# The end of a long convolution: statistics, sums and roundings moved between three engines

## The chip, the cores and the metric

The kernel runs on one core of a Trainium2 chip. A core has a matrix engine (TensorE, PE in the profile; PEld is its loading of weights), a vector engine (VectorE, DVE), a scalar engine (ScalarE, ACT), a general engine (GpSimd, POOL) and a sync engine (SyncE, SP) that issues most transfers. Each engine works through its own instructions in order and waits for others by semaphores. The metric is the device time of one execution in microseconds; less is better.

## The reference, cut to what matters

The model has two layers, each of a cross part and an FFN. The first cross part is a causal convolution over all pairs of features in a head, with `fft_size` twice the length; the change lies at its end and in the first tiles of the FFN after it.

```python
# k = v = ctx, q = layernorm(x); (8, 256, 512) each; 32 heads of 8 rows, length 512
kv  = einsum('bhil,bhjl->bijhl', k_, v_)
y   = irfft(rfft(kv, n=1024) * rfft(ssm_kernel, n=1024))[..., :512]
out = einsum('bijhl,bhil->bjhl', y + kv * D, q_)
x   = x + tanh(g_xattn[0]) * out
# FFN 0: weights rounded to -1, 0, 1 by their mean; activations to 8 bits by row maximum
h   = silu(bitlinear(layernorm(x), w1)) * bitlinear(layernorm(x), w2)
x   = x + tanh(g_ffn[0]) * bitlinear(h, w3)
# then attention over ctx under a mask, and FFN 1 (1-bit weights, activations in groups of 64)
```

`_weight_quant` is `clip(round(w / mean|w|), -1, 1)`; after the rounding the clip of an integer to [-1, 1] equals its sign.

## The kernel before

**The convolution** is done head by head, as a product with a Toeplitz matrix built by the transfers of `load_toep`. Loop variable `h` (lines 716 to 748) runs over the 32 heads; I call one turn a step. For each head the symmetric products of features (36 of 64 pairs) are made on GpSimd (`pair_products`, from the doubled copy that `ctx_twice` makes on ScalarE). TensorE then makes `y` in two halves of PSUM: (h,0) takes 6 matmuls in the trace and (h,1) takes 14. The halves go through a ring of three PSUM tiles (`ps_y`). `half_wrap` on ScalarE copies a few columns of `y` so that a row can be read cyclically; `half_products` on VectorE multiplies by `q` (three instructions, lines 348, 354, 361) into `prod`; `add_halves` on GpSimd adds the two planes of `prod` (line 371); `reduce_terms` on VectorE sums four terms (line 376) into `qT`, one step later. In four heads, `alone = {12, 14, 19, 21}`, GpSimd's adding is left out and VectorE sums all eight terms itself (line 378), in the head's own step.

In step h the order on VectorE is: products (h,1), sum of head h−1, sum of head h if it is lone, products (h+1,0), then the jobs of this step. TensorE makes (h+1,1), then (h+2,0), each into the PSUM tile that the products (h,0) and (h,1) set free.

**Jobs.** Other work is woven into the steps by `job(h, slot, ...)` and run by `run(h, slot)`; slots stand at fixed places of a step ("act", "dve", "pe", "act2", "pool", "late"). The scheduling is manual: program order is each engine's order. Of the jobs, these matter here:
- The rows of `x` are 16 tiles of 128. `ln_moments_of` takes mean and variance of a tile for the normalising of FFN 0, with two instructions on VectorE (lines 116, 117). Tiles are numbered by `order0`; numbers 4 to 7 have their statistics in steps 28 to 31, in slot "dve".
- For the first two tiles `front_norm`, `front_max`, `front_int` and `front_turn` prepare the FFN's input in steps 25 to 29: normalise (ScalarE, line 179), row maximum (VectorE, line 483), round to int8 (ScalarE, line 502), clip and cast (GpSimd, line 506) and a transposing transfer from SP's queue (line 508). The integers lie in one buffer, `i8x` in pool `front1`. In the FFN the same four are run two tiles ahead.
- The weights of FFN 0 are rounded in two passes. `round_w0` (ScalarE, line 447) makes int8 in a ring of three buffers (`pr`), and `clip_w0` (GpSimd, line 454) clips them to bf16. The last matrix has four pieces; they are rounded in steps 27 to 30 and clipped in steps 29, 30, 31, 31.

After step 31 ScalarE loads the table of Silu (line 189), and **FFN 0** (lines 920 to 1005) runs over the tiles t. `up_block` makes two products of 512, 512 and 384 columns in a ring of four PSUM tiles: `pa` is read by silu on ScalarE (line 800), `pb` by the gating on VectorE (line 801). One tile later the hidden row gets its row maximum (line 483), its integers (ScalarE, line 935), a cast on GpSimd (line 951) and a transposing transfer (line 953); two tiles later `down0` multiplies it by the third matrix (line 809). In tile 0, `ln_finish` (three small instructions on VectorE, fourteen on GpSimd) makes the inverse deviations for numbers 4 to 7, and the last head's sum is done at the tile's end (line 984). Its result is read by the transposes of `odd_back` from t = 1 on. Attention and FFN 1 follow and are not touched.

Of the kernel before, what the change touches and what calls it, by code (L numbers as in the profile page):

```python
# [9 lines left out]
F32 = mybir.dt.float32  # L10
BF16 = mybir.dt.bfloat16
F32R = mybir.dt.float32r
I8 = mybir.dt.int8
# [3 lines left out]
AF = mybir.ActivationFunctionType  # L17
ALU = mybir.AluOpType
# [3 lines left out]
P = 128  # L22
B, S, L = 8, 256, 512
NT = B * S // P
NL = L // P
H, HD = 32, 8
# [12 lines left out]
GRP = 4  # L39
# [3 lines left out]
def flamingo_gated_kernel(  # L43
# [15 lines left out]
    nc = tc.nc  # L59

    def pool(stack, name, bufs, **kw):
# [3 lines left out]
    small = pool(ctx, "small", 3)  # L65
# [10 lines left out]
    w0q = [  # L76
        wp_ab.tile([P, NL, FF0], BF16, name="w0_1"),
        wp_ab.tile([P, NL, FF0], BF16, name="w0_2"),
        wp_c.tile([P, NF0, L], BF16, name="w0_3"),
    ]  # L80
    pf = pool(s_front, "front", 2, side="right")
    pf1 = pool(s_front, "front1", 1, side="right")
# [14 lines left out]
    xs = const.tile([P, NT, L], F32, name="xs")  # L97
# [3 lines left out]
    order0 = evens + odds  # L101
# [11 lines left out]
    def ln_moments(mv, j, t):  # L113

        st = small.tile([P, nc.vector.BN_STATS_DIM], F32, tag="st", name="st")
        nc.vector.bn_stats(st, xs[:, t, :])
        nc.vector.bn_aggr(mv[:, j, :], st)
# [19 lines left out]
    def ln_moments_of(got, order, k, tag):  # L137

        g, j = k // GRP, k % GRP
        if g not in got:  # L140
            got[g] = small.tile([P, GRP, 2], F32, tag="mv" + tag, name="mv")
        ln_moments(got[g], j, order[k])

    def ln_finish(got, g, tag):

# [82 lines left out]
    big = pool(s_conv, "p1big", 1)  # L228
    p2 = pool(s_conv, "p1", 2)
# [24 lines left out]
    qT = big.tile([P, NL * B, S], F32, name="qT")  # L254
# [7 lines left out]
    toeps, chs, cxs, kvs, qxs, prods, ys = {}, {}, {}, {}, {}, {}, {}  # L262
# [71 lines left out]
    def half_wrap(h, half):  # L334
        y = ys[h, half]
        nc.scalar.copy(y[:, :, :, 0:W0], y[:, :, :, HD * ND : HD * ND + W0])  # L336
# [36 lines left out]
    def reduce_terms(h, added):  # L373
        prod, o = prods.pop(h), qT[:, :, h * HD : (h + 1) * HD]
        if added:
            nc.vector.tensor_reduce(o, prod[:, 0], AX.X, ALU.add)  # L376
        else:
            nc.vector.tensor_reduce(
                o, prod.rearrange("p k a j d -> p (a j) k d"), AX.XY, ALU.add
            )  # L380

    trs = {}

    def transpose_x(t, xn):
# [18 lines left out]
    FW = [[FF0] * NL, [FF0] * NL, [3 * L, 3 * L, 3 * L, 2 * L]]  # L403
# [37 lines left out]
    w0r = {}  # L441
# [9 lines left out]
    def clip_w0(i, k):  # L451
# [3 lines left out]
            q[:, a : a + n], w0r.pop((i, k))[:, :n], 1.0, -1.0, ALU.min, ALU.max  # L455
        )


    w1a = {}
    N1 = FF1 * L // P // 1024  # L460
# [17 lines left out]
    st0, xn0, i80, am0, x0 = {}, {}, {}, {}, {}  # L478
# [19 lines left out]
        am0[k] = row_max(xn0[k], "x")  # L498

    def front_int(k):  # L500
        i80[k] = pf1.tile([P, L], I8, tag="i8x", name="i8x")
        nc.scalar.activation(i80[k], xn0.pop(k), AF.Copy, scale=am0[k][1])

    def front_turn(k):
# [11 lines left out]
    def job(h, slot, f, *a):  # L516
        jobs.setdefault((h, slot), []).append((f, a))

    def run(h, slot):
        for f, a in jobs.pop((h, slot), []):  # L520
            f(*a)
# [49 lines left out]
    for i, (a, b, c) in enumerate(STEPS0):  # L571
        for k in range(NL):
            job(a + k, "load", load_w0, i, k)
            job(b + k, "act", abs_w0, i, k)
            job(c[k], "act", round_w0, i, k)
            job(c[k] if i < 2 else (29, 30, 31, 31)[k], "pool", clip_w0, i, k)
        job(b + NL - 1, "dve", total_w0, i)
        job(b + NL, "act", spread, i)
        job(b + NL, "dve", mean_w0, i)
    steps1 = [2, 7, 8, 9, 10, 12, 13, *range(15, 19), 18, 19, 20, 21, 23]  # L580
    for k, h in enumerate(steps1):
        job(max(h - 2, steps1[k - 2] if k > 1 else 0), "late", load_w1a, k)
        job(h, "act2", abs_w1, k)
        if k % N1 == N1 - 1:
            i = k // N1
# [8 lines left out]
    for k in range(2):  # L594
# [1 line left out]
        job(26 + k, "dve", front_max, k)  # L596
        job(27 + k, "act", front_int, k)
        job(28 + k, "pool", front_turn, k)
    for k in range(GRP, 2 * GRP):
        job(24 + k, "dve", ln_moments_of, st0, order0, k, "0")  # L600

# [111 lines left out]
    alone = {12, 14, 19, 21}  # L715
    for h in range(H):
        if h + 3 < H:
            load_toep(h + 3)
        if h + 4 < H:
            load_ch(h + 4)  # L720
        run(h, "load")
        if h + 1 < H:
            q_twice(h + 1)
        if h + 3 < H:
            ctx_twice(h + 3)
            pair_products(h + 3)
        half_products(h, 1)
        if h > 0 and h - 1 not in alone:
            reduce_terms(h - 1, True)
        if h in alone:  # L730
            reduce_terms(h, False)
        else:
            add_halves(h)
        if h + 1 < H:
            half_matmuls(h + 1, 1)
        run(h, "act")
        if h + 1 < H:
            half_wrap(h + 1, 1)
            half_products(h + 1, 0)
        run(h, "dve")  # L740
        if h + 2 < H:
            half_matmuls(h + 2, 0)
        run(h, "pe")
        run(h, "act2")
        if h + 2 < H:
            half_wrap(h + 2, 0)
        run(h, "pool")
        run(h, "late")
    assert not jobs
# [17 lines left out]
    p2 = pool(s_mid, "p2", 2, side="right", reuse_waits="tile")  # L767
# [48 lines left out]
    scale = 1.0 / math.sqrt(L)  # L816
# [103 lines left out]
    for t in range(NT + 1):  # L920
        new = t + 2 < NT
        if t < NT:
            hh = p2.tile([P, FF0], F32, tag="hh", name="hh")
        if new:
            front_norm(t + 2)
        if 1 <= t:
            inv, sc = row_max(h_[t - 1], "h")
        if t == NT:
            xT_ = {k: x_transposed(xn_.pop(k)) for k in range(2)}
            xn_[2] = normalised3(2)  # L930
        if t < NT:
            up_block(*x0[t], hh, 0)
        if 1 <= t:
            q = p1.tile([P, FF0], I8, tag="i8h", name="i8h")
            nc.scalar.activation(q, h_.pop(t - 1), AF.Copy, scale=sc)
        if t == NT - 1:
            xn_ = {k: normalised3(k) for k in range(2)}
        if t >= 3:
            residual(order0[t - 3], *d_.pop(t - 3))
        back = BACK.get(t, [])  # L940
        if len(back) == 3:
            sums.append(odd_back(odds[back[0]]))
        if new:
            front_max(t + 2)
        if t < NT:
            up_block(*x0[t], hh, 512)
        if new:
            front_int(t + 2)
        if 1 <= t:
            b = p2.tile([P, FF0], BF16, tag="qh", name="qh0")  # L950
            nc.gpsimd.tensor_scalar(b, q, 127.0, -128.0, ALU.min, ALU.max)
            bT = p_hq.tile([P, NF0, P], BF16, tag="hqT", name="hqT")
            nc.sync.dma_start_transpose(out=bT, in_=b)
            f3 = small.tile([P, 1], F32, tag="f3", name="f3")
            nc.gpsimd.tensor_scalar(f3, inv, gw0, None, ALU.mult)
            hq_[t - 1] = (bT, f3)
        if new:
            front_turn(t + 2)
        for add in sums:
            add()  # L960
        sums = []
        if back:
            sums.append(odd_back(odds[back[-2]]))
        if t >= 2:
            hqT, f3 = hq_.pop(t - 2)
            d_[t - 2] = (down0(hqT), f3)
        if t in FINISH:
            ln_finish(*FINISH[t])

        for k in STATS3.get(t, ()):  # L970
            ln_moments_of(st3, natural, k, "3")
        if t > 0:
            for k in STATS0.get(t, ()):
                ln_moments_of(st0, order0, k, "0")
        if t < NT:
            up_block(*x0.pop(t), hh, 1024)
            h_[t] = hh
        if back:
            sums.append(odd_back(odds[back[-1]]))
        for add in sums:  # L980
            add()
        sums = []
        if t == 0:
            reduce_terms(H - 1, True)
        if t == 3:
            s_conv.close()
            wp1 = pool(ctx, "w1", 1, reuse_waits="tile")
            w1q = [wp1.tile([P, NL, FF1], F32R, name=f"w1_{i + 1}") for i in range(2)]
            p_st = pool(s_att, "w1st", 3, reuse_waits="tile")
        if t == NT - 3:  # L990
            p3 = pool(s_att, "p3", 2, reuse_waits="tile")
            keys, values = {0: load_keys(0)}, {0: load_values(0)}
        for make in signs:
            make()
        signs = []
        if 3 <= t < NT:
            signs = [w1_signs(made + k) for k in range(2)]
            made += 2
        if t == NT - 2:
            bytes_ = {b: load_mask(b) for b in range(2)}  # L1000
        if t == NT - 1:
            negs = {0: key_mask(bytes_.pop(0))}
            gates3 = {0: batch_gate(negs[0])}
        if t == NT:
            negs[1] = key_mask(bytes_.pop(1))
# [90 lines left out]
    for t in range(NT + 2):  # L1096
# [11 lines left out]
        if t == NT:  # L1108
            xn4, q, back = front(1)
# [53 lines left out]
        if t == NT - 4:  # L1163
            ln_some(st4, natural, GRP, "4")
            xn4, q, back = front(0)
# [14 lines left out]
    with ExitStack() as ph:  # L1180
        p2 = pool(ph, "p4", 2, reuse_waits="tile")
# [92 lines left out]
        for t in range(NT):  # L1274
# [6 lines left out]
            if t > 0:  # L1281
                hh = px.tile([P, HW], F32, tag="hh", name="hh4")
                g = up_products(xT, 0)
# [4 lines left out]
                g = up_products(xT, 1)  # L1288
# [7 lines left out]
            g = up_products(xT, 2)  # L1296
# [5 lines left out]
            g = up_products(xT, 3)  # L1302
# [76 lines left out]
```

## Time and profile before

| | us |
|---|---|
| three runs | 744.36, 744.26, 742.74 |
| their median | 744.26 |
| the profiled execution | 743.63 |
| its span | 741.8 |
| mean granted clock of TensorE | 0.998 of full |

The span is what the profiler saw from the first to the last instruction; the execution's own time holds 1.83 us more around it. The convolution ends near 188 us, FFN 0 near 312, attention near 400, and FFN 1 takes the rest. The profile page's first part, busy time with its share of the span and the number of instructions:

```profile
PE 712.2 (96%) x3172; PEld 527.8 (71%) x3172; DVE 606.8 (82%) x1234; ACT 362.3 (49%) x638; POOL 255.9 (34%) x360
```

Of its second part, the row of GpSimd: 40 slices of the span, in tenths of a slice.

```profile
POOL 2888988988875435443200010000200002000000
```

GpSimd's work lies almost wholly in the first half, and in the convolution's slices it is nearly full. The page's average over the whole span hides this, as it hides any stage: the change touches only some steps between 80 and 206 us, and these have to be looked at by themselves.

### The profile page before, as it was taken

The numbers are of one execution on the slowest core, as the hardware profiler recorded it, in microseconds if no ns is written. First come the engines' busy times: TensorE is split into PE (matmuls) and PEld (weight loads), VectorE is DVE, ScalarE is ACT, GpSimd is POOL, SyncE is SP. The second block draws the span as 40 slices with busy tenths as digits, with TensorE's granted clock in tenths as the row PEclk, the third lists the DMA queues.
The fourth block names the chain that finished last, engine by engine and source line by source line (L and its number), as shares of the span: only waits on it lengthen the run. The fifth ranks groups of instructions, "written<-read, shape, count | busy, mean of one in ns | idle before, by whom it ended". The sixth has DMA issues, their size and how long they took to land.

```text
span 741.8 us, 10045 instructions
## 1 busy us (share of the span) xinstructions
PE 712.2 (96%) x3172; PEld 527.8 (71%) x3172; DVE 606.8 (82%) x1234; ACT 362.3 (49%) x638; POOL 255.9 (34%) x360
## 2 busy tenths in 40 slices
PE   4999999999899999899989999999999999999997
PEld 3777777776454444556657888888888888888885
DVE  5799878998888888877767999888889888778965
ACT  5477877756677886767742233222223322222322
POOL 2888988988875435443200010000200002000000
PEclk9999999999999999999999999999999999999999
DMA  5675775921145667686602555455534545553443
GB/s 193 224 230 169 183 263 190 287 79 31 22 89 135 151 139 173 152 278 192 206 35 46 109 123 124 90 114 110 115 85 105 113 92 123 109 111 85 109 88 85
DMA packets 150444, 99.36 MB, mean 134 GB/s; under 512 B 84280, under 2 KB 128312, under 8 KB 150392
## 3 DMA queue, kind: packets, MB, share of 16 engines
q1 hardware_dynamic: 149608, 98.38, 51.7%
q0 software_dynamic: 256, 0.26, 0.5%
q8 instruction: 25, 0.41, 0.2%
q14 instruction: 27, 0.22, 0.1%
q10 hardware_dynamic: 528, 0.08, 0.1%
HBM read 75.58 MB, written 5.03 MB: 109 GB/s over the span
## 4 chain that ended last, share of the span: by engine, by line
PE 64%; DVE 5%; DMA 2%; POOL 2%; issue 1%; ACT 1%; SPq 0%; DVEq 0%; POOLq 0%
PE po L1254 16%; PE pb L1076 15%; PE pa L1076 15%; PE po L809 5%; PE pb L792 4%; PE pa L792 4%; PE po L904 3%; PE ps L875 2%; DMA w1st<-in_L_w3t 1%; DMA sT<-d 1%; DMA hqT<-qh 1%; PE tr L867 1%; DVE qT L376 0%; DVE prod L348 0%; DMA w1st<-in_L_w2t 0%
## 5 line engine op out<-in xcount | busy, mean ns | idle before, releaser
L326 PE MATMUL y<-kv,toep 128*128 128x288 f32 x640 | 162.4, 410 | 4.0 <-DVE prod L361 2.7
L326 PEld LDWEIGHTS y<-kv,toep 128*128 128x128 f32 x640 | 120.2, 192 | 37.6 <-ACT qx L290 3.0
L1084 ACT ACTIVATE sl<-pa,wmean 128x512 f32<-128x512 f32 x64 | 44.0, 689 | 187.6 <-PE pa L1076 187.6
L1076 PE MATMUL pa<-w,hi 128*128 128x512 f32 x256 | 100.7, 393 | 0.0
L1254 PE MATMUL po<-w,lo 128*128 128x512 f32 x256 | 100.0, 391 | 0.0
L1076 PE MATMUL pb<-w,hi 128*128 128x512 f32 x256 | 99.8, 390 | 0.1
L1254 PE MATMUL po<-w,hi 128*128 128x512 f32 x256 | 99.7, 390 | 0.0
L1076 PE MATMUL pa<-w,lo 128*128 128x512 f32 x256 | 99.7, 389 | 0.0
L1076 PE MATMUL pb<-w,lo 128*128 128x512 f32 x256 | 99.7, 389 | 0.0
L159 POOL TENSOR_TENSOR nwt<-rstd 128x4 f32<-128x4 f32 x33 | 6.5, 198 | 247.2 <-DVE rstd L154 245.3
L303 POOL TENSOR_TENSOR kv<-cx 128x1024 f32<-128x1024 f32 x32 | 60.6, 1893 | 32.9 <-ACT cx L290 30.4
L371 POOL TENSOR_TENSOR prod<-prod 128x1024 f32<-128x1024 f32 x28 | 66.2, 2366 | 2.7 <-DVE prod L361 2.7
L792 PEld LDWEIGHTS <-xqT 128*128 128x128 bf16 x384 | 37.4, 97 | 41.5 <-issue 4.5
L1051 ACT CAST hi<-v 128x512 fp32r<-128x512 f32 x64 | 39.1, 622 | 48.0 <-DVE v L1244 48.0
L1088 DVE SCALAR_TENSOR_TENSOR hh<-pb,wmean,sl 128x512 f32<-128x512 f32 x64 | 47.7, 745 | 15.4 <-PE pb L1076 15.4
L1254 PEld LDWEIGHTS po<-w,lo 128*128 128x128 f32 x256 | 48.1, 188 | 10.8 <-DVE lo L1056 1.0
L1076 PEld LDWEIGHTS pb<-w,hi 128*128 128x128 f32 x256 | 48.0, 188 | 10.6 <-DVE hh L1088 0.5
L1076 PEld LDWEIGHTS pa<-w,hi 128*128 128x128 f32 x256 | 48.1, 188 | 10.4 <-issue 0.5
L1076 PEld LDWEIGHTS pa<-w,lo 128*128 128x128 f32 x256 | 48.1, 188 | 10.3 <-issue 0.5
L1076 PEld LDWEIGHTS pb<-w,lo 128*128 128x128 f32 x256 | 48.1, 188 | 10.0
L1254 PEld LDWEIGHTS po<-w,hi 128*128 128x128 f32 x256 | 48.0, 188 | 9.9
L348 DVE TENSOR_TENSOR prod<-y,qx 128x512 f32<-128x512 f32 x64 | 43.6, 681 | 10.7 <-ACT y L336 6.8
(141 smaller groups left out, 1327.3 us busy)
## 6 DMA issues: line engine op xcount, KB each, us to landing
sT<-d SPq DMA_DIRECT2D x64, 256.0 KB
toep<-ssm_skip SPq DMA_DIRECT2D x31, 256.0 KB
ch<-in_ctx_heads SPq DMA_DIRECT2D x32, 128.0 KB
w1a<-in_L_w1t SPq DMA_DIRECT2D x8, 512.0 KB
w1a<-in_L_w2t SPq DMA_DIRECT2D x8, 512.0 KB
w1st<-in_L_w1t SPq DMA_DIRECT2D x16, 256.0 KB
w1st<-in_L_w2t SPq DMA_DIRECT2D x16, 256.0 KB
cT<-in_ctx_t SPq DMA_DIRECT2D x8, 512.0 KB
```

The costliest lines, as they stand in the source:

```text
L303: nc.gpsimd.tensor_tensor(kv[:, :, 0 : ND * HD].rearrange("p a (i d) -> p a i d", d=ND), cx[:, :, 0:HD].unsqueeze(3).to_broadcast([P, NL * ...
L326: nc.tensor.matmul(y[:, k, :, W0 : W0 + NPAIR], toeps[h][:, d * P : (d + 1) * P], kvs[h][:, mi * B : (mi + 1) * B, :].rearrange("p b n -> ...
L348: nc.vector.tensor_tensor(prod[:, 0, r, :, :], yv[:, :, W0 : W0 + ND * HD].rearrange("p a (i d) -> p a i d", d=ND), view(q, [HX, n], [1, H ...
L371: nc.gpsimd.tensor_tensor(flat[0], flat[0], flat[1], ALU.add)
L792: nc.tensor.matmul(pp[:, :fw], xqT[:, c, :], w0q[i][:, c, f0 : f0 + fw], start=(c == 0), stop=(c == NL - 1),)
L809: nc.tensor.matmul(po, hqT[:, c, :], w0q[2][:, c, :], start=(c == 0), stop=(c == NF0 - 1))
L904: nc.tensor.matmul(po, eT[:, c, :], cN[:, c, :], start=(c == 0), stop=(c == S // P - 1))
L1051: nc.scalar.copy(hi, v)
L1076: nc.tensor.matmul(pp, xT[k][:, c, :], w1q[i][:, c, f0 : f0 + 512], start=(c == 0 and k == 0), stop=(c == NL - 1 and k == 1),)
L1084: nc.scalar.activation(sl, pa, AF.Silu, scale=wmean1[:, 0:1])
L1088: nc.vector.scalar_tensor_tensor(hh, pb, wmean1[:, 1:2], sl, op0=ALU.mult, op1=ALU.mult)
L1254: nc.tensor.matmul(po, hT[b][k][:, c, :], w1q[2][:, b * NL + c, :], start=(b == 0 and c == 0 and k == 0), stop=(b == NB - 1 and c == NL - ...
```

## The change

Five things are done.
1. The sum of a lone head moves one step later, to the place where other heads have theirs.
2. The integers of tile number 1 get a buffer of their own, in pool `p1big`.
3. The statistics of numbers 5, 6 and 7 are taken on ScalarE, in slot "late" of steps 29, 30 and 31: a pass that sums the row, a one-column scaling, a pass that sums squares of the deviations, two more one-column scalings. Number 4 stays on VectorE.
4. The last head's sum is done on GpSimd, in two additions, in step 31 after the adding of its halves and ahead of the step's clip; `prod`'s second plane holds the half sums.
5. The last piece of the last weight matrix is clipped on ScalarE as a sign, at the end of tile 0, in place of GpSimd in step 31.

```diff
+    def moments_by_act(got, order, k, tag, junk):
+        g, j = k // GRP, k % GRP
+        mean, var = got[g][:, j, 0:1], got[g][:, j, 1:2]
+        v = xs[:, order[k], :]
+        st = small.tile([P, nc.vector.BN_STATS_DIM], F32, tag="st", name="st")
+        nc.scalar.activation(junk, v, AF.Identity, accum_out=st[:, 0:1])
+        nc.scalar.activation(st[:, 1:2], st[:, 0:1], AF.Copy, scale=-1.0 / L)
+        nc.scalar.activation(junk, v, AF.Square, bias=st[:, 1:2], accum_out=st[:, 2:3])
+        nc.scalar.activation(mean, st[:, 0:1], AF.Copy, scale=1.0 / L)
+        nc.scalar.activation(var, st[:, 2:3], AF.Copy, scale=1.0 / L)
...
+    def reduce_last(h):
+        prod, o = prods.pop(h), qT[:, :, h * HD : (h + 1) * HD]
+        half = prod[:, 1, :, :, 0:2]
+        nc.gpsimd.tensor_tensor(half, prod[:, 0, :, :, 0:2], prod[:, 0, :, :, 2:4], ALU.add)
+        nc.gpsimd.tensor_tensor(o, half[..., 0], half[..., 1], ALU.add)
...
+    def clip_by_act(i, k):
+        n, a = FW[i][k], sum(FW[i][:k])
+        q = w0q[i].rearrange("p c f -> p (c f)")
+        nc.scalar.activation(q[:, a : a + n], w0r.pop((i, k))[:, :n], AF.Sign)
...
     def front_int(k):
-        i80[k] = pf1.tile([P, L], I8, tag="i8x", name="i8x")
+        i80[k] = (big if k == 1 else pf1).tile([P, L], I8, tag="i8x", name="i8x")
...
-            job(c[k] if i < 2 else (29, 30, 31, 31)[k], "pool", clip_w0, i, k)
+            if (i, k) != (2, 3):
+                job(c[k] if i < 2 else (29, 30, 31)[k], "pool", clip_w0, i, k)
...
-    for k in range(GRP, 2 * GRP):
-        job(24 + k, "dve", ln_moments_of, st0, order0, k, "0")
+    def first_by_act(k):
+        junk = p2.tile([P, L], F32, tag="xn", name="junk")
+        moments_by_act(st0, order0, k, "0", junk)
+
+    job(28, "dve", ln_moments_of, st0, order0, GRP, "0")
+    for k in range(GRP + 1, 2 * GRP):
+        job(24 + k, "late", first_by_act, k)
...
-        if h > 0 and h - 1 not in alone:
-            reduce_terms(h - 1, True)
-        if h in alone:
-            reduce_terms(h, False)
-        else:
+        if h > 0:
+            reduce_terms(h - 1, h - 1 not in alone)
+        if h not in alone:
             add_halves(h)
...
+        if h == H - 1:
+            reduce_last(h)
         run(h, "pool")
...
         if t == 0:
-            reduce_terms(H - 1, True)
+            clip_by_act(2, 3)
```

## The prediction

> **What bounds the kernel now.** I read the busy time by stage first, then the chain that ended last, then the timeline of the two stretches that the change touches. The rows by stage (window in us, its length, then busy us and count of PE, weight loads, DVE, ACT and POOL, granted clock, DMA share, GB/s):
>
> ```profile
> 82.00:128.00 46.00, 44.64 (x194) 34.71 (x193) 38.04 (x67) 35.69 (x66) 40.97 (x29) 1.00 0.69 217
> 128.00:171.00 43.00, 41.96 (x187) 32.83 (x185) 40.23 (x85) 29.80 (x55) 37.30 (x27) 1.00 0.56 171
> 171.00:188.00 17.00, 14.37 (x56) 10.06 (x56) 14.83 (x33) 9.26 (x15) 14.32 (x12) 1.00 0.15 31
> 188.00:206.00 18.00, 15.73 (x80) 7.86 (x79) 16.18 (x31) 11.11 (x18) 14.97 (x26) 1.00 0.23 36
> 206.00:312.00 106.00, 103.91 (x523) 52.24 (x524) 91.42 (x183) 81.91 (x115) 53.92 (x106) 1.00 0.61 138
> ```
>
> TensorE is full nearly everywhere; only 171 to 206, the convolution's end and the first tiles of the FFN, leaves it 4.9 us idle (17.00 − 14.37 plus 18.00 − 15.73). After 206 it has 2% of slack, so time won or lost before 206 goes through to the end. The chain of waits agrees: from 179 to 195 it is almost all DVE, from 206 all PE, and between them runs GpSimd, then the transpose of the first hidden tile (start, length, what):
>
> ```profile
> 199.51 0.23 POOL nmr L165
> 199.74 0.89 issue
> ...
> 200.68 1.36 POOL qh L951
> ...
> 202.06 4.05 DMA hqT<-qh
> ...
> 206.16 2.55 PE po L809 x11
> ```
>
> So 206.16 is the gauge: what moves it moves the end.
>
> **Part 1, lone sums in the next step.** A lone step now does two sums on DVE before it may do the products that free TensorE's next PSUM tile. The timeline (start, length, engine, line, in brackets the idle time before it):
>
> ```profile
> 87.02 1.22 DVE L376 TENSOR_REDUCE qT<-prod 128x256 f32<-128x1024 f32 x1 [1.06 <-POOL prod L371]
> 88.16 2.27 DVE L378 TENSOR_REDUCE qT<-prod 128x256 f32<-128x2048 f32 x1
> ...
> 91.86 9.94 PE L326 MATMUL y<-kv,toep 128*128 128x288 f32 x40 [1.13 <-DVE prod L361]
> 102.03 13.33 PE L326 MATMUL y<-kv,toep 128*128 128x288 f32 x54 [0.23 <-DVE prod L361]
> ```
>
> Step 12: with the 2.27 sum gone, products (13,0) start at 88.16 and end at 89.5; TensorE had been done at 85.72 + 5.02 = 90.74 and goes straight on: **1.13 won**. The sum lies in step 13 between products (13,1), 89.7 to 91.0, and (14,0), which then end at 94.5; TensorE wants them after 20 matmuls of 0.2485 from 90.74, at 95.71: no new stall. Step 14, alike: **0.23 won**; sum 14 in step 15 makes (16,0) end at 105.0, wanted at 105.65. Steps 19 and 21 hide stalls too (0.48 and 0.56 of PE idle at 128.76 and 140.14). But there DVE, 40.23 of 43.00 busy, has as much work as before and only one listed wait after 137 (0.28): I count nothing, and keep 0 to 1.0 for the range. No DMA moves by itself; the loads of a step follow its buffers. Part 1: −1.36, at worst −0.3 if a load of the context heads becomes late (cx waited 1.21 for one at 129.93).
>
> **Part 2, the tail**, in the old clock, part 1 taken off at the end. The rows that carry it:
>
> ```profile
> 178.10 0.72 ACT L502 ACTIVATE i8x<-xn,sc 128x512 int8<-128x512 f32 x1 [3.95 <-POOL qx L506]
> 179.07 0.69 DVE L348 TENSOR_TENSOR prod<-y,qx 128x512 f32<-128x512 f32 x1 [1.60 <-ACT y L336]
> 187.25 1.28 ACT L189 ACT_TABLE_LOAD   x1
> 189.36 0.67 ACT L800 ACTIVATE sl<-pa,f 128x512 f32<-128x512 f32 x1
> 191.83 0.75 DVE L801 SCALAR_TENSOR_TENSOR hh<-pb,f,sl 128x512 f32<-128x512 f32 x1
> 192.35 2.46 POOL L454 TENSOR_SCALAR w<-w0r 128x1536 bf16<-128x1536 int8 x2
> 194.14 0.70 DVE L150 TENSOR_SCALAR nwv<-mv 128x4 f32<-128x4 f32 x1
> ```
>
> *The second buffer* lets integers of tile 1 be made at 174.1; ACT then copies wraps as TensorE delivers them, and DVE's 1.60 goes: products (29,1) start at 177.4. What is late next is TensorE: its 20 matmuls from 176.80 end at 181.9, the last 14 at 185.4 instead of 186.85. So of 1.60 about 1.4 is left.
>
> *Three rows' statistics.* DVE loses 3 × 0.89 (0.70 + 0.18, spaced). ACT gains five instructions a row and two accumulator reads, each result needed by the next. Nearest rows, an accumulating pass and a waiting pair:
>
> ```profile
> 329.56 0.63 ACT L780 ACTIVATE w<-w1st 128x512 fp32r<-128x512 f32 x1 [1.72 <-DMA w1st<-in_L_w3t]
> 330.23 0.63 ACT L782 ACTIVATE w1st<-w1st 128x512 f32<-128x512 f32 x1
> 330.76 0.18 ACT L782 ACTIVATION_READ_ACCUMULATOR w1st<-w1st 128x1 f32 x1
> ```
>
> The pass's read ends 0.72 after its start; an instruction that waits for the one before starts 0.04 after its end (329.56 + 0.63, 330.23); a one-column activation takes 0.20 (188.54). Identity and read 0.72; copy 0.76 to 0.96; Square from 1.00, with a column as bias 0.72, its read done at 1.82; last copies, next row may start at **2.0**. Both ends: 1.9 (no waits) and 3.16 (nothing overlaps: .63 + .19 + .29 + .80 + .19 + .29 + .29 and six gaps of 0.08). I take 2.0, built from measured spacings.
>
> ACT from TensorE's 181.9: wrap 0.2, row 5 2.0, qx 0.5, rounding 1.05, wrap 0.2, rows 6 and 7 4.0, table load 1.28, one column 0.1, normalise 0.7: first silu at **192.05** where it was 189.36. These follow each other without a gap, so ACT is the new bound; every 0.1 in a row costs 0.3. Behind row 5 waits qx of head 31, so products (31,0) start at 185.0 with DVE idle 1.1; nothing that ends last hangs on it, as (31,1) are done by 187.0 and PSUM for the FFN comes free at 186.4.
>
> Here the skill speaks against the change: "ScalarE: Activation LUTs", What ACT_TABLE_LOAD costs, gives a switch of sets 2.66 us, 1.38 of it a drain. Row 187.25 shows 1.28, 0.02 after the wrap before it (186.93 + 0.30), and the next instruction at 188.54. By the page's sum the silu would come at 193.4; by the row at 192.05. The number of switches is unchanged and Square and Sign belong to the sets loaded; I take the row.
>
> From there: DVE's first gating 192.8 (was 191.83), its second 1.64 later, 194.4. Then three small operations: 194.14 took 0.70, until the two POOL roundings ended at 194.81; the same line takes 0.16 at 224.10. "SBUF — State Buffer", Who interferes with whom, says the pair of ports is an exclusive lock of the first to issue. Now POOL's rounding of tile 2 (0.61) falls at 195.15: without the lock these would end at 195.65, with it at 195.85; I take the latter. Third gating 195.9 (was 195.45).
>
> *The last sum on GpSimd* removes DVE's 1.20 at 195.98. On POOL: 128x512 as L914, 1.25; 256 columns between L309 (0.46) and that, 0.66: 1.9, from 190.1, after the last adding of halves. ACT takes one rounding of 1.06 (L420, 1024 columns) off POOL, so POOL is free by 193.5, before the integers of tile 2 at 195.1. The sum's reader, the transpose at 198, does not notice. Costs 0; with the cover gone, 1.9. The rounding on ACT lies at 195.5 to 196.6, where ACT waited 2.99 for DVE: 0.
>
> So row maximum h0 starts at 196.4 (197.10), the next gating 198.35 (199.04), the integers on ACT 198.45 (199.12), POOL's cast 200.05 (200.68; its Newton steps end 200.0), first down matmul 205.5 (206.16): **−0.63**. The transpose of tile 2 leaves at 195.8, with 4.05 (as hqT) is there at 199.9, wanted at 200.5.
>
> **Sum.** −1.36 − 0.63 = −2.0. The profiled execution took 743.63 (span 741.8): 741.6. The three runs' median, 744.26, lies 0.63 higher; I set the time midway, **741.9**.
>
> **Rivals.** Each with the same 0.3 for the runs. (a) *ACT's rows eat the gain.* At 2.5 a row the silu comes 1.5 later and the tail is +0.87: with part 1 −0.5, 743.4. For it: seven dependent instructions a row; against: the 0.04 gaps. (b) *Slower*, the same place: at the serial 3.16 a row the silu comes 3.5 later, tail +2.85. With part 1 at only −0.3 that is 746.5; with it at −1.36, 745.4. From 3.16 a row (or 2.8 with part 1 at −0.3) the sum passes +1.5 and it decides for slower. For it: the first silu gates DVE, PSUM and the transposes in turn, and no row shows accumulating Identity or Square. (c) *More than forecast*: stalls of steps 19 and 21 count too, −1.0: 740.9. For it: TensorE would be ahead at 145 and POOL's adds, which DVE waits for at 156.87, come earlier; against: DVE's full share. (d) *The change does not do what it says*: part 1's stall is replaced by POOL's add of head 13 (94.52 to 96.88), which leaves the tail's gain alone: 743.3. The order of DVE's instructions does show the sums one step later.
>
> **Chances.** Forecast 0.47, its own range 740.6 to 743.0; (a) and (d) 0.27; (b) 0.14; (c) 0.12. About 0.2%, 1.5 us, is what a measurement tells from no change. Faster: 0.40 of the forecast's 0.47 and all of (c), 0.52; within: 0.07 and 0.24, 0.31; slower: 0.14 and 0.03, 0.17. Range 740.2 to 745.0: (c) and most of (a), with the runs' own spread, and half of (b).
>
> **What would show it.** No PE idle over 0.3 at the two lone steps 12 and 14; no wait of ACT for POOL near 177; a row's seven ACT instructions in 2.0; first silu about 6 us after the last wrap (two rows 4.0, load and normalising 2.1); last sum on POOL near 1.9; first down matmul about 2.0 earlier than 206.16. A row above 2.5, or PE idle moved to steps 13, 15, 20 or 22, proves me wrong.

## The result, and the profile after

| | before | after |
|---|---|---|
| first comparison: median, range | 744.17 (742.74 to 744.72), 6 runs | 741.36 (740.73 to 742.91), 6 runs |
| its ratio, 95% interval | | 0.9966 [0.9953, 0.9979] |
| second comparison, another chip | 744.28, 31 runs | 742.71 (739.96 to 744.35), 22 runs |
| its ratio, 95% interval | | 0.9981 [0.9969, 0.9992] |
| span of the first profile | 741.8 | 740.1 |

The change makes the kernel 0.2 to 0.3% faster; the forecast was 741.9. The rows by stage of the kernel after (window, its length, busy us and count of PE, weight loads, DVE, ACT and POOL, granted clock, DMA share, GB/s), the same windows as before:

```profile
82.00:128.00 46.00, 46.00 (x202) 36.14 (x201) 40.34 (x72) 36.20 (x68) 41.30 (x29) 1.00 0.71 224
...
188.00:206.00 18.00, 14.02 (x74) 7.47 (x74) 12.48 (x26) 15.16 (x22) 13.21 (x27) 1.00 0.25 36
```

TensorE is now full from 82 to 128 (46.00 of 46.00, was 44.64). From 188 to 206 it is busy less than before (14.02, was 15.73), DVE too (12.48, was 16.18), and ACT more (15.16, was 11.11): work has moved to ACT, and the chain below shows that it bounds the end of the convolution. TensorE's timeline (start, length, engine, line, instruction; in brackets the idle time before it and what ended it) shows the same two things:

```profile
85.53 28.01 PE L338 MATMUL y<-kv,toep 128*128 128x288 f32 x114
...
169.39 5.09 PE L338 MATMUL y<-kv,toep 128*128 128x288 f32 x20 [0.82 <-DVE rstd L126]
...
190.64 0.81 PE L822 MATMUL pa<-w,xqT 128*128 128x384 bf16 x4 [2.82 <-ACT sl L830]
...
203.88 2.33 PE L839 MATMUL po<-w,hqT 128*128 128x512 bf16 x10 [0.82 <-DMA hqT<-qh]
```

The stalls of steps 12 and 14 are gone: 114 matmuls run in one piece. A new wait of 2.82 us for ACT's silu has come. Why ACT is late is read from its own timeline, one row's statistics (number 7) and what follows it:

```profile
185.79 0.61 ACT L150 ACTIVATE junk<-xs 128x512 f32<-128x512 f32 x1
...
187.61 0.20 ACT L154 ACTIVATE mv<-st 128x1 f32<-128x1 f32 x1
187.81 1.28 ACT L201 ACT_TABLE_LOAD   x1
...
189.92 1.24 ACT L830 ACTIVATE sl<-pa,f 128x512 f32<-128x512 f32 x2
```

The row before it began at 183.85, this one at 185.79: a row takes 1.94 us, seven instructions nose to tail, then the table load with nothing between. The chain that ended last says who holds the end (start, length, what):

```profile
190.02 0.58 ACT sl L830
190.62 0.75 DVE hh L831
...
193.33 0.56 DVE rstd L166
...
197.57 0.21 POOL nmr L176
198.17 1.36 POOL qh L981
199.56 4.27 DMA hqT<-qh
```

From 179.88 to 190.62 it is ACT (before it was DVE there), then DVE, GpSimd's fourteen small steps, the cast and the transpose.

**Four marks.** The runs of one kernel spread by several us (before: 741.47 to 746.91 in the second comparison), so the experiments are read by marks inside each profile. M0 is the start of the 20 matmuls at 80.43 in before and 80.25 after (the instructions ahead of it are alike), M1 that of the 20 which the trace lists as released by DVE's line 126 (171.48 and 169.39), M2 GpSimd's cast of the first hidden row (200.68 and 198.17), M3 its first down matmul (206.16 and 203.88). All distances in us, from the profiles of all fourteen executions:

| profile | M0 to M1 | M1 to first silu | M1 to M2 | M2 to M3 | M0 to M3 |
|---|---|---|---|---|---|
| before | 91.05 | 17.88 | 29.20 | 5.48 | 125.73 |
| after | 89.14 | 20.53 | 28.78 | 5.71 | 123.63 |
| after, second comparison (e9) | 89.90 | 20.54 | 28.79 | 5.65 | 124.34 |
| e1_lone | 89.59 | 17.62 | 28.91 | 5.78 | 124.28 |
| e2_tail | 91.44 | 20.54 | 28.78 | 5.65 | 125.87 |
| e3_dve_rows | 89.41 | 16.32 | 27.47 | 5.45 | 122.33 |
| e4_gaps | 89.72 | 16.27 | 26.87 | 4.97 | 121.56 |
| e5_one_buffer | 88.83 | 21.45 | 29.71 | 5.39 | 123.93 |
| e6_sum_dve | 89.29 | 20.54 | 29.64 | 6.06 | 124.99 |
| e7_clip_pool | 89.89 | 20.53 | 28.78 | 5.88 | 124.55 |
| e8_two_clips | 88.84 | 16.27 | 25.44 | 5.05 | 119.33 |
| e8 again (e10) | 89.51 | 16.28 | 25.48 | 4.96 | 119.95 |
| e11_clip_only | 89.72 | 20.53 | 28.79 | 5.40 | 123.91 |
| e12_dve_rows_clip | 89.63 | 16.31 | 26.17 | 5.57 | 121.37 |

M1 to M2 comes again to 0.01 for the same kernel (28.78 and 28.79) and to 0.04 for e8. That is fine enough to price one edit of the tail; the times alone are not. The other distances repeat less well: M0 to M1 differs by 0.76 between the two profiles of after and by 0.67 between those of e8, and from M3 to the end of the span the profiles took 534.3 to 537.9. So the prediction's "what moves it moves the end" can be checked only in the medians of many runs.

### The profile page after: what moved, and what is told of

It reads as the page before. It is cut to its first block, busy times and chain, and to the rows that moved or that the text cites. A ratio compares the mean times of both kernels' runs of the same rounds, so it can differ in the third digit from the quotient of the medians.

```text
span 740.1 us, 10062 instructions
## 1 busy us (share of the span) xinstructions
PE 711.0 (96%) x3172; PEld 528.3 (71%) x3172; DVE 603.5 (82%) x1227; ACT 368.6 (50%) x660; POOL 256.2 (35%) x361
## 4 chain that ended last, share of the span: by engine, by line
PE 85%; DVE 5%; ACT 3%; POOL 2%; DMA 1%; issue 1%; DVEq 0%; ACTq 0%
PE y L338 19%; PE po L1284 16%; PE pa L1106 16%; PE pb L1106 16%; PE po L839 4%; PE pb L822 4%; PE pa L822 4%; PE po L934 3%; PE ps L905 2%; DMA hqT<-qh 1%; PE tr_back L413 1%; PE tr L405 1%; DVE am L507 1%; POOL neg L878 0%; ACT w L810 0%
```

## The experiments

My theory (A in the expectations, which were refined from batch to batch): part 1 carries the gain; the tail's four edits nearly cancel, because three rows on ACT at its very end cost what the others win. The rivals (B) are written into each. The first four ran on one chip (before: 744.1, 35 runs), e5 to e8 on a second (743.12, 59 runs), e9 to e12 on a third (744.28, 31 runs).

**e1_lone**: before, with part 1 alone.

```diff
-        if h > 0 and h - 1 not in alone:
-            reduce_terms(h - 1, True)
-        if h in alone:
-            reduce_terms(h, False)
-        else:
+        if h > 0:
+            reduce_terms(h - 1, h - 1 not in alone)
+        if h not in alone:
             add_halves(h)
```

> The kernel before with part 1 alone: the sum of a lone head one step later, nothing else. Theory A (part 1 carries the gain; the traces show the convolution 1.9 us ahead at step 27, and the tail follows rigidly): 1.9 us less than before, ratio 0.9975, the products of (27,1) near 165.4 in place of 167.35, and no PE idle over 0.3 us at steps 12 and 14. Theory B (VectorE's full steps 22 to 31 swallow the lead, and the gain belongs to the tail): under 0.5 us, ratio above 0.9993.

Measured: 741.79 (18 runs), ratio 0.9972 [0.9959, 0.9984]; M0 to M1 89.59. TensorE runs through the two steps in one piece here too:

```profile
86.10 28.02 PE L326 MATMUL y<-kv,toep 128*128 128x288 f32 x114
```

Part 1 alone brings as much as the whole change, within the intervals.

**e2_tail**: after, with the same lines put back, so all but part 1.

> The changed kernel with part 1 taken back: second buffer, three rows' statistics and last rounding on ScalarE, last sum on GpSimd stay. Theory A: the tail is nearly even, first down matmul 0.2 to 0.6 us earlier than in the kernel before, ratio 0.9992 to 0.9997. Theory B: the tail carries the gain, 2 us or more, ratio 0.9973 or less.

Measured: 744.0 (14 runs), 0.9998 [0.9986, 1.001]; M1 to M2 is that of after (28.78), M0 to M3 that of before (125.87). The tail's edits by themselves give nothing that the time shows.

**e3_dve_rows**: after, with the three rows' statistics on DVE as before.

```diff
-    job(28, "dve", ln_moments_of, st0, order0, GRP, "0")
-    for k in range(GRP + 1, 2 * GRP):
-        job(24 + k, "late", first_by_act, k)
+    for k in range(GRP, 2 * GRP):
+        job(24 + k, "dve", ln_moments_of, st0, order0, k, "0")
```

> The changed kernel with the three rows' statistics back on VectorE in steps 29 to 31, all else as changed. Theory A (the rows on ScalarE are a loss, since they stand between the last wrap and the first silu; the first silu comes 4 us earlier without them, VectorE's own 2.7 us takes back a part): the first gating 2.3 us earlier than in the changed kernel, first down matmul about 1.3 us earlier, 740.1, ratio to before 0.9948. Theory B (VectorE is the bound of the tail and the rows' leaving it is a gain): 1 to 2.7 us slower than the changed kernel, ratio 0.998 to 1.0003.

Measured: 740.04 (8 runs), 0.9949 [0.9932, 0.9966]. The first silu comes 4.21 earlier after M1 (16.32), the cast only 1.31 (27.47). What took the rest shows in DVE's timeline of this kernel, and in GpSimd's:

```profile
188.21 0.18 DVE L117 BATCH_NORM_AGGREGATE mv<-st 128x2 f32<-128x6 f32 x1
188.41 0.75 DVE L830 SCALAR_TENSOR_TENSOR hh<-pb,f,sl 128x512 f32<-128x512 f32 x1
...
190.92 1.34 DVE L164 TENSOR_SCALAR nwi<-nwv 128x4 int32<-128x4 int32 x1
```

```profile
190.77 1.47 POOL L472 TENSOR_SCALAR w<-w0r 128x1536 bf16<-128x1536 int8 x1
```

The first gating waits until DVE has made the last row's statistics (188.41; the silu began at 186.09 and takes 0.67), and line 164 takes 1.34 where it took 0.17 in after: GpSimd's clip ran from 190.77 to 192.24, and this ended with it. So the rows are a net loss on ACT at that place, and behind them stand DVE and GpSimd.

**e4_gaps**: after, with each row's two passes split over ACT's idle times in steps 26, 28 and 29. (`first_sum` holds the first pass and its scaling, `first_squares` the rest of `moments_by_act`; both are left out here.)

```diff
...
-    for k in range(GRP + 1, 2 * GRP):
-        job(24 + k, "late", first_by_act, k)
+    for k, h in ((GRP + 1, 26), (GRP + 2, 28), (GRP + 3, 29)):
+        job(h, "act", first_sum, k)
+        job(h, "act2", first_squares, k)
```

> The changed kernel with the same statistics on ScalarE, but each row in two halves in the gaps where ScalarE waits for TensorE: the sum ahead of the first wrap, the squares ahead of the second, in steps 26, 28 and 29. Theory A (not the rows' work but their place at the end of ScalarE's queue costs): first silu about 4 us earlier than in the changed kernel, first down matmul about 2 us earlier, then bound by GpSimd's Newton steps: 739.3, ratio to before 0.9937. Theory B (wraps come late in steps 26 to 29 and VectorE waits for them): no faster than the changed kernel, ratio 0.9966 or more, with VectorE waits for y of 0.5 us or more in these steps.

Measured: 741.18 (8 runs), 0.9953 [0.9937, 0.997]; the silu 4.26 earlier, as expected, the cast 1.91. GpSimd's timeline:

```profile
190.09 1.46 POOL L472 TENSOR_SCALAR w<-w0r 128x1536 bf16<-128x1536 int8 x1
...
196.23 0.23 POOL L177 TENSOR_SCALAR nmr<-nmr 128x4 f32<-128x4 f32 x1
196.54 1.36 POOL L1002 TENSOR_SCALAR qh<-i8h 128x1408 bf16<-128x1408 int8 x1
```

The integers of the first hidden row were done at 194.20 (started 192.73, 1.47 long), but the cast stands behind the clip and the fourteen small steps and starts at 196.54. With ACT out of the way GpSimd's queue is the bound, as theory A had it. Theory B did not show: the only wait of DVE for a wrap that the trace lists between 150 and 184 is 0.38. From M0 the first down matmul comes 2.07 earlier than in after, as expected, and yet the time missed the expected 739.3. In the profiled run that is a loss right behind the mark: TensorE, after waiting 2.19 us, ran the eleven down matmuls in 4.24 us instead of 2.55 (last section).

**e5_one_buffer**, **e6_sum_dve**, **e7_clip_pool**: after, each with one part undone.

```diff
-        i80[k] = (big if k == 1 else pf1).tile([P, L], I8, tag="i8x", name="i8x")
+        i80[k] = pf1.tile([P, L], I8, tag="i8x", name="i8x")
```

```diff
-        if h == H - 1:
-            reduce_last(h)
...
         if t == 0:
+            reduce_terms(H - 1, True)
             clip_by_act(2, 3)
```

```diff
-            if (i, k) != (2, 3):
-                job(c[k] if i < 2 else (29, 30, 31)[k], "pool", clip_w0, i, k)
+            if True:
+                job(c[k] if i < 2 else (29, 30, 31, 31)[k], "pool", clip_w0, i, k)
...
-            clip_by_act(2, 3)
```

> The changed kernel with one buffer for the integers again. Theory A (ScalarE is the tail's bound, and its wait of 4 us for GpSimd pushes all that follows): that wait is back near 172, the first silu 1.1 us later than in the changed kernel, 742.5, ratio to before 0.998. Rival (ScalarE stands idle between 171 and 180 anyway, so the wait costs nothing): ratio 0.9966 as the changed kernel.

> The changed kernel with the last head's sum back on VectorE at the end of tile 0, all else as changed. Theory A (VectorE's sum of 1.2 us stands between the third gating and the maximum of the first hidden row): that maximum 1.2 us later, first down matmul 1.0 us later, 742.4, ratio 0.998. Rival (VectorE waits 4.2 us for the first silu and has time to spare): no change, 0.9966.

> The changed kernel with the last rounding (1024 columns) back on GpSimd in step 31. Theory A: it falls into GpSimd's wait of 2.0 us before the integers of tile 2, and on ScalarE it lay in a wait too, so no change, ratio 0.9966 within 0.0005. Rival (GpSimd is late for the rounding of tile 2, and VectorE's small operations wait for it): 1 us slower, 0.998.

Measured, 22 runs each: 742.74, 0.9991 [0.9979, 1.0002]; 741.67, 0.9983 [0.9971, 0.9994]; 741.96, 0.9978 [0.9967, 0.9989]. After itself is 0.9966 on one chip and 0.9981 on another, so these times separate none of the three. The marks do: at M2 the buffer is worth 0.93 (29.71), the sum on GpSimd 0.86 (29.64), the clip nothing (28.78), each with the other edits in place.

**e8_two_clips**: e4_gaps (its lines are not repeated), and a second piece of the weights (1536 columns) clipped on ACT between the second silu and the integers of tile 2, in place of GpSimd in step 31.

```diff
-            if (i, k) != (2, 3):
-                job(c[k] if i < 2 else (29, 30, 31)[k], "pool", clip_w0, i, k)
+            if (i, k) not in ((2, 2), (2, 3)):
+                job(c[k] if i < 2 else (29, 30)[k], "pool", clip_w0, i, k)
...
             up_block(*x0[t], hh, 512)
+        if t == 0:
+            clip_by_act(2, 2)
```

> The rows' statistics in ScalarE's gaps as in e4_gaps, and the third piece's clip (1536 columns) on ScalarE as well, between the second silu and the integers of tile 2. In e4_gaps the first hidden row's cast waited 2.3 us for GpSimd's Newton steps, and TensorE 2.2 us for the transpose. Theory A: GpSimd gets to tile 2 and to the Newton steps 1.5 us earlier, the first down matmul comes near 200.0 (201.5 in e4_gaps), 738.5 or less, ratio 0.9925 to 0.994. Rival (the bound is ScalarE: its 1.5 us more delay the silu of tile 1): as e4_gaps or slower, 0.995 or more.

Measured: 736.22 (735.32 to 738.23, 6 runs), 0.9909 [0.9886, 0.9932]; the cast 3.34 before that of after (25.44). Its chain of waits:

```profile
184.97 2.36 POOL prod L383
187.41 1.04 POOL prod L397
...
193.88 0.23 POOL nmr L177
...
194.19 1.36 POOL qh L1004
195.58 3.62 DMA hqT<-qh
```

From the last adding of halves to the cast GpSimd has no gap longer than 0.1: up to the cast the tail is now bound by it alone. TensorE is busy 16.64 of 18.00 us between 188 and 206.

**e9_after** and **e10_two_clips_again**: after and e8 unaltered, side by side.

> The changed kernel itself once more, as the anchor of the other three. If the small differences of e5, e6 and e7 were real, it is 0.9966 of the kernel before again (0.995 to 0.998), first silu near 189.9 and first down matmul near 203.9. If they were the spread of chips and profiles, it comes at 0.998 or above.

> e8_two_clips once more, beside the changed kernel. Theory A (ACT's rows at the end and GpSimd's chain behind the clip hold the tail): 0.991 of before again and 0.994 to 0.995 of the changed kernel; first down matmul near 199.2 and no matmul at half clock behind it. Theory B (its 736 was a lucky one, most of it from the attention stage where it happened not to lose clock): 0.994 or above, with half-clock matmuls near 300 or 376.

Measured: 742.71, 0.9981 [0.9969, 0.9992], and 736.33 (735.41 to 737.81, 6 runs), 0.9899 [0.9878, 0.992]. e8 is 1% faster than before and 0.9% faster than the changed kernel beside it (736.33 to 742.71). Its profiled run, 737.81, has the eleven slow matmuls near 300 that theory A had ruled out (last section), so that part of the expectation missed; e9 takes away the small differences in time of e5 to e7.

**e11_clip_only**: after with e8's second clip on ACT, the rows left at the end. **e12_dve_rows_clip**: e3_dve_rows with the same clip on ACT.

> The changed kernel with only the second clip moved to ACT, its three rows left at the end. Theory A: GpSimd waited 2.0 for ACT's integers there anyway, so the clip's 1.47 was hidden; on ACT it ends 0.3 after the scale is ready: 0 to +0.4 against the changed kernel (ratio to before the same to 0.0005 higher), first silu 189.9, first down matmul 203.8 to 204.3. Theory B (GpSimd's work itself held the tail): 0.9945 or below, first down matmul 1.5 earlier.

> The changed kernel with the statistics back on DVE and the second clip on ACT. Theory A (GpSimd binds as soon as ACT's rows are out of the way): in e3_dve_rows GpSimd's last Newton step ended 197.16 and DVE's line 164 waited 1.2 for its clip; without the clip the cast comes about 1.5 earlier, first down matmul near 201.2: 0.002 below e3's 0.9949, 0.993. It stays behind e8_two_clips by 1.5 to 2 (0.002), which has three rows less on DVE. Theory B (the clip does nothing here either): 0.995, first down matmul 202.7.

Measured: e11 740.06 (10 runs), 0.995 [0.9932, 0.9968], and e12 739.06 (6 runs), 0.9934 [0.9911, 0.9957]. By the marks theory A holds in both, though e11's ratio lies nearer to theory B's 0.9945 than to that of after, 0.9981. With the rows at ACT's end the clip does nothing for the cast (28.79), since GpSimd waits for ACT all the more:

```profile
193.04 0.61 POOL L530 TENSOR_SCALAR qx<-i8x 128x512 bf16<-128x512 int8 x1 [3.46 <-ACT i8x L526]
```

(3.46; in after that wait is 2.00.) Without the rows there it is worth 1.30 (27.47 to 26.17, e3 to e12), and with them in the gaps 1.43 (26.87 to 25.44, e4 to e8). That e11's median is yet 2.65 below e9's its tail does not explain. In the two profiles (spans 739.3 and 741.8) 1.36 of the 2.5 lies in M0, 79.46 and 80.82, ahead of anything that differs, 0.43 between M0 and M3 and 0.71 behind M3; whether the medians share that is open.

## Why the prediction was right

**Part 1** was forecast at −1.36. Over the stretch of the two stalls TensorE takes 27.99 (85.53 to 113.52) where it took 29.62 (85.72 to 115.34): 1.63. The 0.27 more fit, nearly, the last matmul ahead of each stall, which the trace shows with its whole 0.41 instead of the spacing of 0.25 (2 × 0.16). Steps 19 and 21, counted at nothing, did win at first: at the group that began at 145.50 before and 142.16 after, the lead is 3.34, 3.16 without the difference of M0. But by M1 1.25 of that is given back. DVE does not follow: it is busy 24.95 of the 26.00 us from 145 to 171, and no wait of it is listed there. TensorE waits 0.82 at M1, where before it waited 0.24, and the 26 matmuls ahead of it take 7.21 where they took 6.55. This is the reason for which rival (c) was held down ("DVE's full share"), and it held. M0 to M1 is 89.46 in the mean of the twelve profiles with part 1, 91.05 and 91.44 in the two without: −1.8. No profile of the one kind comes within 1.1 of the other. The forecast was low by 0.4.

**The tail**'s steps were met closely up to the third gating. A row: 2.0 forecast, 1.94 measured. With the convolution's lead of 2.1 in this profile taken off, the first silu was due at 189.95 and came at 189.92, the first gating at 190.7 (190.62), the third at 193.8 (193.80). (The terms that the prediction lists for ACT add up to 191.93, not to its 192.05; this changes nothing below.) The table load took 1.28 and started at 187.81, as the instruction before it ended: no drain, as in the row of before, and not the 2.66 of the page that the prediction quoted. The lock between DVE and GpSimd came again, in line 166: 0.56 from 193.33 beside GpSimd's cast of tile 2 (193.25, 0.61 long), 0.17 in e3. The sum on GpSimd took 1.73 (1.9 forecast; two additions of 1.04 and 0.64, lines 397 and 398).

At the cast the tail wins 0.42 (29.20 to 28.78; against e1 only 0.13), at the down matmul 0.19 (34.68 to 34.49), for 0.63 forecast. The shortfall arises behind the third gating, in small steps. The row maximum needs that gating's result and starts 0.64 after it (due at 194.3, it came at 194.44); the forecast gave it the 0.5 at which, in before, a sum followed that did not need it. The cast, which in before waited for ACT's integers, now waits for GpSimd's fourteen steps: the integers are done at 197.95, the last step at 198.09, the cast starts at 198.17. And the distance from the cast to the matmul, carried over as 5.48, is 5.71. It is 5.78 in e1, which has the tail of before, so nothing says that the tail's edits lengthened it.

Single edits, each taken out of the changed kernel, show how they share the cast. The rows' net price, which the prediction did not give apart, is 1.31 (e3); the second buffer is worth 0.93 (e5), the sum 0.86 (e6), the clip 0 (e7). 1.31 − 0.93 − 0.86 = −0.48, against −0.42 measured. The prediction's 1.4 for the buffer and 1.20 for the sum are not refuted by this: it reckoned the buffer ahead of the rows. At the first silu the edits do not even add up: 4.21 for the rows (e3) less 0.92 for the buffer (e5) is 3.29, and the silu comes 2.65 later than in before.

**The total** was met by luck in part: part 1 brought some 0.4 more than forecast and the tail some 0.4 less. Between M0 and M3 the two profiles of after win 2.10 and 1.39, the medians of the two comparisons 2.81 and 1.57, for a forecast of 2.0. The times do not show the tail's share: e1, with part 1 alone, is 2.31 below its before, and e2, with the tail's edits alone, 0.1. They confirm part 1; for the tail there are only the marks.

**The rivals.** (a), ACT's rows eating the gain, is true of the tail's gain: they take back some three quarters of what buffer and sum bring there, though not at the 2.5 a row that it supposed. (c): M0 to M1 went 0.4 past the forecast of part 1, not 1.0. (b) needed 3.16 a row and had 1.94. (d) did not show: no idle time of TensorE at step 13. What the prediction did not see is that the same rows fit into ACT's gaps: it priced the move as given and did not ask what stood free earlier.

## What to carry to other kernels

Work moved to an idle engine is priced by where in that engine's queue it lands: against the same rows on DVE, the three rows on ACT cost 1.31 us at the cast where everything waits for ACT's next instruction (e3 to after), and win 0.60 there when they lie in ACT's gaps a few steps before (e3 to e4). When one engine is relieved, follow the chain to the next one at once: moving a clip off GpSimd was worth 0 at the cast with ACT as the bound, and 1.3 to 1.4 us without. Where runs spread by 0.6% and an edit is worth 0.1%, measure between marks in the trace.

## What was not expected of the hardware

**TensorE can drop to half clock behind a wait of only 2 us.** The eleven down matmuls near 300, in e8's second profile (e10) and in e12's:

```profile
300.91 4.24 PE L860 MATMUL po<-w,hqT 128*128 128x512 bf16 x11 [1.95 <-DMA hqT<-qh]
```

```profile
302.87 2.55 PE L838 MATMUL po<-w,hqT 128*128 128x512 bf16 x11 [2.00 <-DMA hqT<-qh]
```

After 1.95 us of waiting they took 4.24, at a granted clock of 0.86 between 296 and 308; after 2.00 us they took 2.55, at 1.00. In all profiles a wait of 1.94 to 2.19 ahead of the down matmuls occurs six times, three of them with slow matmuls; of seven such waits of 1.57 to 1.89 none has them. The wait for the first silu, in e2 and in e9:

```profile
192.56 1.44 PE L824 MATMUL pa<-w,xqT 128*128 128x384 bf16 x4 [2.83 <-ACT sl L832]
```

```profile
191.98 0.81 PE L822 MATMUL pa<-w,xqT 128*128 128x384 bf16 x4 [2.83 <-ACT sl L830]
```

Of the seven profiles that have this wait (2.82 to 3.16) four show slow matmuls behind it and a granted clock of 0.91 between 188 and 206, and three none. While it lasts, four matmuls of 512 columns take 1.70 (192.38 to 194.08 in e5) where 0.86 is usual. So a wait of about 2 to 3 us brings a risk of another 1.1 to 1.7 us of matmuls: 1.69 in the down matmuls, 1.42 in e5, e6 and e11 and 1.08 in e2 over the groups after the silu.

Whether it costs time depends on what follows. In e4 all of it went on: from the first down matmuls to the next ones it took 10.13 (201.51 to 211.64), in e3 8.45. Behind the silu later waits took it up: e2 and e11, with slow matmuls, start the first down matmul 34.43 and 34.19 after M1, after and e9, without, 34.49 and 34.44. The times of e4 go with the clock: its two runs with a mean clock of 0.998 took 738.13 and 740.21, its six others, at 0.997 and below, 741.2 in the median; this mean is of the whole kernel, with the attention's drops in it. The Trainium skill, "TensorE: Matmul & The Clock Gate", section HAM oscillation — how this bites in real kernels, warns of gaps above about 3.4 us; here shorter ones were enough. That its window runs freely, as the same page says under What's actually happening, would make it a matter of chance; no run here shows the window, so what decides between two equal waits stays open.

**The start is not the same in each execution.** The first six matmuls of the convolution, near 12.6, took 2.12 to 3.09 us over the fourteen profiles, where the next six take 1.62, and M0 lies between 79.46 and 80.82, although the instructions are alike up to there. This alone is 1.4 us, as much as the forecast of part 1, and a reason to measure from M0. Its cause is open: the granted clock between 10 and 16 reads 1.00 both in the profile with 2.12 (e11) and in one with 3.09 (e9).
